# A cross-attention loop on one core: VectorE makes the low parts of the queries and the fourth maximum ahead of the transposition of probabilities

## The chip, the core and the metric

The kernel runs on one core of a Trainium2 chip. The metric is the device time of one execution in microseconds. Five engines work from queues of their own, each in the order in which the program gives it instructions: TensorE (PE; its weight loads are shown as PEld), VectorE (DVE), ScalarE (ACT), GpSimd (POOL), and SyncE (SP), which here only issues DMAs. An engine stops at an instruction whose inputs, or whose output buffer, are not ready, and everything behind it in its queue stops too.

## The reference

The input `x` is 32 batches of 512 queries with 640 channels; the context is 32 batches of 77 keys with 1024 channels. There are 20 heads of 32 channels. Only the text part of the context exists (77 keys), so the other three attentions of the source have no keys. Cut to what is computed:

```python
q = x @ to_q_w                                   # 32 x 512 x 640, 20 heads of 32
k, v = ctx @ to_k_w, ctx @ to_v_w                # 32 x 77 x 640
s = einsum('bhqd,bhkd->bhqk', q, k) / sqrt(32)
out = merge(softmax(s) @ v) @ to_out_w + to_out_b + x
```

All is float32. The kernel keeps float32 precision on PE by splitting operands into a high part (rounded to the PE's reduced format) and a low part (the remainder): three products instead of one.

## The kernel before

A first stage (some 280 us of the span) projects keys and values of all batches and stores them, split, in DRAM. Then comes the main loop of 160 *slots*: slot n works on batch b = n div 5 and on chunk j = n mod 5, that is on four heads (128 channels) and all 512 queries. The slots are pipelined by hand; the order of instructions in the code is the order in each engine's queue. `slot(n)` issues work for several chunks at once:

- **Queries of the next chunk.** `queries(n+1)` is 15 matmuls (L442) into the one PSUM bank `pq`, six between the first and second scores, nine between the second and third. `split_q(n+1)` makes the high part with ScalarE (L453), copies it to the other half of the partitions with POOL (two of L457), and makes two low parts with VectorE (two of L459). All three kinds are needed by the first scores of slot n+1.
- **Scores and exponentials of this chunk.** `scores(n, t)` for the four query tiles t = 0 to 3: three matmuls each (L477, one against `kb`, two against `kc`), and a VectorE reduction for the negated maxima (L485, "nm"). There are three score banks. `exps(n, t)`: four exponentials of ScalarE (L495), one a head, with their sums; they write the probabilities `pn` (two buffers).
- **Normalization and transposition of the chunk before.** `sums(n-1)` is a reciprocal on VectorE (L505). `normalize(n-1)` is one POOL product over all probabilities (L510). `transpose_p(n-1)` is one VectorE transposition in 32 x 32 blocks into the single buffer `z` (L517), and four SP DMAs of `z` to the scratch tensor `pd` (L524).
- **Values two slots on.** `load_p` brings `pd` back as `raw`, in another layout, with two SP DMAs (L533, L534): that of slot m + 2 brings the chunk m. In slot m + 3 `cast_p`, `rest_p` and `last_p` split it: ScalarE casts (L541, L547), a VectorE difference (L548), a POOL difference (L555). `values` is six matmuls (L569) into `pa`. `sum_a` adds the halves: a ScalarE copy (L580) and two VectorE sums (L582). In the slot after, `high_a` (ScalarE, L589) and `low_a` (VectorE, L594) split the result.
- **Output projection.** `piece` issues 24 matmuls a slot (L612) for a batch behind, in two groups, into two banks `po`. `finish` adds a closed bank to the residual with bias `xr` (VectorE, L641) and stores it (SP). The residual is loaded by SP (`load_residual`, L601, in j = 1 to 4) and gets its bias from POOL (`add_bias`, L605), in j = 2 and 3 ahead of L555, else behind the query copies.
- **Input of the next batch.** SP loads `xs` (L253, in slots j = 4), VectorE transposes it (L257, one in j = 0, two in j = 1, one in j = 2), ScalarE and POOL split it (L264, L265, two chunks in j = 2, three in j = 3).

So on VectorE a slot of the steady loop reads, before the change: maximum 0, L548, reciprocal, L594, maximum 1, xr sums, maximum 2, **transposition (L517), two low parts (L459), maximum 3**, xr sums, sums of the values (L582); with the transpositions of x where they belong. On PE: scores 0, six query matmuls, scores 1, nine query matmuls, scores 2, output projection, values, scores 3, output projection. On ScalarE: L541, L589, L547, exponentials 0 and 1, query copy (L453), exponentials 2, copies of x, L580, exponentials 3. On POOL: bias, L555, normalization, query copies, low parts of x, bias.

The flag `has_out` is true where an output projection of an earlier batch belongs to the slot (n = 7 and up); `ahead` is false only in the last slot.

Of the kernel before, what the change touches and what calls it, by code (L numbers as in the profile page):

```python
# [51 lines left out]
def kernel(  # L52
# [410 lines left out]
    def scores(n, t):  # L463
        b, j = divmod(n, NC_)
        g = GROUP_OF[j]
        qt, (kb, kc) = qts[n % 2], kbs[g]
        jg = j - GROUPS[g][0]
        sc = ps.tile([P, S], F32, tag="sc", name="sc", bufs=3)
        half = KCOLS // 2
        for m, (cols, keys_) in enumerate(  # L470
            (
                (slice(0, KCOLS), kb[:, jg]),
                (slice(0, half), kc[:, jg, 0]),
                (slice(half, KCOLS), kc[:, jg, 1]),
            )
        ):
            nc.tensor.matmul(  # L477
                sc[:, cols],
                qt[:, m, t * P : (t + 1) * P],
                keys_,  # L480
                start=(m == 0),
                stop=(m == 2),
            )
        nm = main.tile([P, HPC], F32, tag="nm", name="nm", bufs=3)
        nc.vector.tensor_reduce(  # L485
            nm, sc[:, :KCOLS].rearrange("p (h k) -> p h k", k=NKEY), AX.X, ALU.max, negate=True
        )
        return sc, nm
# [14 lines left out]
    def sums(n):  # L503
        rs = main.tile([P, NQ * HPC], F32, tag="rs", name="rs", bufs=2)
        nc.vector.reciprocal(rs, sms.pop(n))  # L505
        return rs
# [7 lines left out]
    def transpose_p(n):  # L514

        pn = pnb[n % 2]
        nc.vector.transpose(  # L517
            z.rearrange("p b t j -> p t b j"),
            pn.rearrange("p (t h) k -> p t (h k)", t=NQ).rearrange("p t (b i) -> p t b i", i=Q),
        )  # L520
        pd = dram.tile([(NBLK + 2) * Q, S], F32, tag="pd", name="pd", bufs=6)
        rows = pd[: NBLK * Q].rearrange("(b i) q -> i b q", i=Q)
        for a in range(4):
            nc.sync.dma_start(  # L524
                rows[:, :, a * P : (a + 1) * P],
                z[a * Q : (a + 1) * Q].rearrange("p b t j -> p b (t j)"),
            )
        pds[n] = pd
# [8 lines left out]
    def cast_p(n):  # L537

        raw = raws[n]
        pp = late[0].tile([P, 5, S], FPR, tag="pp", name="pp", bufs=1)  # L540
        nc.scalar.copy(pp[:, 0:2, :], raw[:, 0:2, :])  # L541
        pps[n] = pp

    def rest_p(n):

        raw, pp = raws[n], pps[n]
        nc.scalar.copy(pp[:64, 4, :], raw[:64, 2, :])  # L547
        nc.vector.tensor_tensor(  # L548
            pp[:, 2:4, :], raw[:, 0:2, :], pp[:, 0:2, :].bitcast(F32), ALU.subtract
        )  # L550

    def last_p(n):

        raw, pp = raws.pop(n), pps[n]
        nc.gpsimd.tensor_tensor(  # L555
            pp[64:, 4, :], raw[:64, 2, :], pp[:64, 4, :].bitcast(F32), ALU.subtract
        )
# [26 lines left out]
    def high_a(n):  # L584
        if n >= N - NC_ + 1:
            at = xpool[0].tile([P, 2, S], FPR, tag="xt", name="at", bufs=7)
        else:
            at = late[0].tile([P, 2, S], FPR, tag="at", name="at", bufs=8)
        nc.scalar.copy(at[:, 0, :], pas[n][:, 0])  # L589
        ats[n] = at  # L590
# [13 lines left out]
    def add_bias(b, t):  # L604
        nc.gpsimd.tensor_tensor(xrs[b, t], xrs[b, t], bias, ALU.add)  # L605
# [29 lines left out]
    def finish():  # L635

        while closed:
            b, t, h = closed.pop(0)
            xr = xrs[b, t]
            cols = slice(h * HALF, (h + 1) * HALF)  # L640
            nc.vector.tensor_tensor(  # L641
                xr[:, cols], pos.pop((b, t, h))[:, :HALF], xr[:, cols], ALU.add
            )
            if (b, t) == (B - 1, NQ - 1):
                nc.sync.dma_start(out[b, t * P : (t + 1) * P, cols], xr[:, cols])
            elif h == 1:
                nc.sync.dma_start(out[b, t * P : (t + 1) * P, :], xr)
# [23 lines left out]
    def refill(b, j, part):  # L671

        heads = range(2 * part, 2 * part + 2)
        segments = SEGMENTS[4 * part : 4 * part + 4]
        if j == 0:
            load_keys(b, 1, heads)
        elif j == 1:
            load_values(b, 0, segments)
        elif j == 2 and b + 1 < B:
            load_keys(b + 1, 0, heads)  # L680
        elif j == 3:
            load_values(b, 1, segments)

    def slot(n, beside=()):
        b, j = divmod(n, NC_)
        ahead, more = n + 1 < N, b + 1 < B
        back, first = PIECES[j]
        bo_, has_out = b - back, b >= back
        xsplits = SPLIT_X.get(j, ((), ())) if more and n > LATE else ((), ())
        turns = TRANSPOSE_X.get(j, ((), (), ())) if more and b else ((), (), ())  # L690
        if b == 1 and j < 2:
            turns = (((), (), ()), ((0, 1), (2,), ()))[j]
        taken = takes.get(n)

        filling = taken is not None and not has_out
        if not filling:
            refill(b, j, 0)
        if taken is not None:
            cast_p(taken)
        if n - 1 in takes:  # L700
            high_a(takes[n - 1])
        bias_now = j in BIAS and b >= BIAS[j][0]
        if bias_now and (j in (2, 3) or not ahead):
            add_bias(b - BIAS[j][0], BIAS[j][1])
        s = scores(n, 0)
        if taken is not None:
            rest_p(taken)
        rs = sums(n - 1) if n else None
        if taken is not None:
            last_p(taken)  # L710
        if n:
            normalize(n - 1, rs)
        if n - 1 in takes:
            low_a(takes[n - 1])
        exps(n, 0, *s)
        if ahead:
            queries(n + 1, 0, 2)
        s = scores(n, 1)
        if n - LAG + 1 in pds and n > LATE:
            load_p(n - LAG + 1)  # L720
        if filling:
            refill(b, j, 0)
        if n == NC_:
            load_x(b + 1, (2, 3))
        for k in WO.get(n, ()):
            nc.sync.dma_start(wos[0][:, k].bitcast(F32), wo_dram[:, k].bitcast(F32))
        refill(b, j, 1)
        finish()
        if j == 4 and b and b + 2 < B:
            load_x(b + 2, (0, 1))  # L730
        if j in RESIDUAL and b >= RESIDUAL[j][0]:
            load_residual(b - RESIDUAL[j][0], RESIDUAL[j][1])
        exps(n, 1, *s)
        for i in turns[0]:
            transpose_x(b + 1, i)
        if ahead:
            queries(n + 1, 2, NC_)
        s = scores(n, 2)
        if not ahead:
            exps(n, 2, *s)  # L740
            piece(bo_, first)
            s = scores(n, 3)
        early = ahead and has_out and j in (0, 3)
        if early:
            piece(bo_, first)
            finish()
        if n and has_out:
            transpose_p(n - 1)
        if ahead:
            split_q(n + 1)  # L750
            if bias_now and j not in (2, 3):
                add_bias(b - BIAS[j][0], BIAS[j][1])
            exps(n, 2, *s)
        if n and not has_out:
            transpose_p(n - 1)
        if j == 4 and b + 2 < B:
            load_x(b + 2, (0, 1) if not b else (2, 3))
        for c in xsplits[0]:
            split_x(b + 1, c)
        if not ahead:  # L760
            exps(n, 3, *s)
            normalize(n, sums(n))
            finish()
            piece(bo_, first + 1)
            values(taken)
            sum_a(taken)
            return
        if has_out:
            if not early:
                piece(bo_, first)  # L770
        else:
            s = scores(n, 3)
        if taken is not None:
            values(taken)
        if len(beside) > 0:
            context_values(LAST, beside[0], psv)
        if has_out:
            s = scores(n, 3)
        finish()
        for i in turns[1]:  # L780
            transpose_x(b + 1, i)
        if taken is not None:
            sum_a(taken)
        for c in xsplits[1]:
            split_x(b + 1, c)
        exps(n, 3, *s)
        if len(beside) > 1:
            context_values(LAST, beside[1], psv)
        if has_out:
            piece(bo_, first + 1)  # L790
        for i in turns[2]:
            transpose_x(b + 1, i)
# [141 lines left out]
```

## Time and profile before

| | |
|---|---|
| median of the runs | 2037.02 us (3 runs, 2031.57 to 2038.48) |
| profiled execution | 2031.54 us |
| its span, first to last instruction | 2029.8 us |
| granted PE clock, mean | 0.992 |
| PE busy | 1913.5 us (94%) |
| PE weight loads busy | 1677.6 us (83%) |
| VectorE busy | 1559.7 us (77%) |
| ScalarE busy | 1533.9 us (76%) |
| POOL busy | 1237.7 us (61%) |
| DMA moved | 437.69 MB, 216 GB/s in the mean |

The lines of a profile name the line of the kernel, the engine, the operation and its tiles. A group's line gives the number of instructions, their busy time, the mean time of one, and the idle time of the engine in front of them with what ended it. A line of the waits gives who waited for whom: total us, number of waits, the longest. A line of the timeline gives the start in us from the span's beginning, the duration, the engine, the line, the operation with its tiles, how many instructions are merged, and in brackets the idle time before with its releaser. "issue" stands where the profile shows no releaser. Matmuls overlap in their pipelines, so two starts say more than one duration.

### The profile page before, as it was taken

The numbers are of one execution on the slowest core, as the hardware profiler recorded it, in microseconds if no ns is written. First come the engines' busy times: TensorE is split into PE (matmuls) and PEld (weight loads), VectorE is DVE, ScalarE is ACT, GpSimd is POOL, SyncE is SP. The second block draws the span as 40 slices with busy tenths as digits, with TensorE's granted clock in tenths as the row PEclk, the third lists the DMA queues.
The fourth block names the chain that finished last, engine by engine and source line by source line (L and its number), as shares of the span: only waits on it lengthen the run. The fifth ranks groups of instructions, "written<-read, shape, count | busy, mean of one in ns | idle before, by whom it ended". The sixth has DMA issues, their size and how long they took to land.

```text
span 2029.8 us, 37658 instructions
## 1 busy us (share of the span) xinstructions
PE 1913.5 (94%) x10332; PEld 1677.6 (83%) x10332; DVE 1559.7 (77%) x2494; ACT 1533.9 (76%) x6210; POOL 1237.7 (61%) x1030
## 2 busy tenths in 40 slices
PE   9999997999999999999999999999999999999998
PEld 7787886788888888888888888888888888888887
DVE  4444346788888888888888888888888888888885
ACT  3232237888888888888888888888888888888883
POOL 1201156676667766766666667766776667666663
PEclk9999999999999999999999999999999999999999
DMA  9878878888888888889888888888888888889875
GB/s 187 183 178 228 192 185 209 217 225 223 218 226 220 219 225 225 229 216 230 219 219 225 215 230 226 217 226 224 226 225 223 217 226 217 223 218 233 225 195 161
DMA packets 586305, 437.69 MB, mean 216 GB/s; under 512 B 212400, under 2 KB 494448, under 8 KB 586096
## 3 DMA queue, kind: packets, MB, share of 16 engines
q1 hardware_dynamic: 580944, 420.78, 82.7%
q0 software_dynamic: 5056, 14.34, 2.6%
q8 instruction: 85, 1.39, 0.3%
q14 instruction: 124, 1.02, 0.2%
q10 hardware_dynamic: 96, 0.16, 0.0%
HBM read 253.48 MB, written 181.64 MB: 214 GB/s over the span
## 4 chain that ended last, share of the span: by engine, by line
POOL 24%; DVE 19%; DMA 18%; issue 13%; ACT 12%; PE 11%; SPq 3%; DVEq 0%; POOLq 0%; ACTq 0%
POOL pn L510 14%; POOL pp L555 9%; PE pk L191 6%; DVE qt L459 6%; DMA raw<-pd 5%; DMA pd<-z 5%; ACT pn L495 4%; DVE z L517 4%; DMA xs<-in_x_dram 3%; DVE pa L582 3%; ACT pp L541 3%; PE pv L191 3%; DVE nm L485 2%; ACT at L589 2%; DMA out_dram<-xr 2%
## 5 line engine op out<-in xcount | busy, mean ns | idle before, releaser
L495 ACT ACTIVATE pn<-sc,nm 128x77 f32<-128x77 f32 x2560 | 802.8, 335 | 227.5 <-DVE nm L485 221.3
L612 PE MATMUL po<-wo_s,at 128*128 128x320 f32 x3840 | 641.6, 315 | 5.9 <-DVE xr L641 3.1
L442 PE MATMUL pq<-xt,wq_s 128*128 128x512 f32 x2400 | 620.3, 399 | 0.0
L612 PEld LDWEIGHTS po<-wo_s,at 128*128 128x128 f32 x3840 | 569.8, 190 | 17.8 <-DVE xr L641 6.8
L495 ACT ACTIVATION_READ_ACCUMULATOR pn<-sc,nm 128x1 f32 x2560 | 546.0, 213 | 0.0
L442 PEld LDWEIGHTS pq<-xt,wq_s 128*128 128x128 f32 x2400 | 429.7, 190 | 76.1
L555 POOL TENSOR_TENSOR pp<-raw,pp 64x512 fp32r<-64x512 f32 x160 | 216.2, 1352 | 387.6 <-ACT pp L547 279.3
L517 DVE STREAM_TRANSPOSE z<-pn 128x1280 f32<-128x1280 f32 x160 | 241.9, 1512 | 205.2 <-POOL pn L510 205.1
L510 POOL TENSOR_TENSOR pn<-pn,rs 128x1232 f32<-128x1232 f32 x160 | 364.4, 2277 | 14.2 <-DVE rs L505 1.8
L477 PE MATMUL sc<-kc,qt 128*128 128x154 f32 x1280 | 257.8, 263 | 79.8 <-DVE qt L459 50.4
L477 PEld LDWEIGHTS sc<-kc,qt 128*128 128x128 f32 x1280 | 218.4, 188 | 131.6 <-issue 69.3
L485 DVE TENSOR_REDUCE nm<-sc 128x4 f32<-128x308 f32 x640 | 291.5, 464 | 14.1 <-PE sc L477 8.8
L605 POOL TENSOR_TENSOR xr<-xr,bias 128x640 f32<-128x640 f32 x128 | 200.5, 1568 | 112.6 <-DMA xr<-in_x_dram 86.1
L569 PE MATMUL pa<-pp,vb 128*128 128x512 f32 x960 | 252.0, 397 | 4.4 <-POOL pp L555 3.0
L582 DVE TENSOR_TENSOR pa<-pa,aw 64x512 f32<-64x512 f32 x320 | 222.5, 695 | 21.6 <-ACT aw L580 11.2
L548 DVE TENSOR_TENSOR pp<-raw,pp 128x1024 fp32r<-128x1024 f32 x160 | 198.1, 1238 | 40.8 <-ACT pp L541 40.7
L265 POOL TENSOR_TENSOR xt<-xs,xt 128x512 fp32r<-128x512 f32 x160 | 202.6, 1285 | 36.7 <-ACT xt L264 28.8
L459 DVE TENSOR_TENSOR qt<-pq,qt 64x512 fp32r<-64x512 f32 x320 | 214.5, 670 | 9.5 <-ACT qt L453 4.6
L457 POOL CAST qt<-qt 64x512 fp32r<-64x512 f32 x320 | 195.4, 611 | 19.7
L477 PE MATMUL sc<-kb,qt 128*128 128x308 f32 x640 | 195.9, 306 | 9.0 <-ACT pn L495 4.3
L569 PEld LDWEIGHTS pa<-pp,vb 128*128 128x128 f32 x960 | 173.7, 188 | 35.1 <-POOL pp L555 3.9
L580 ACT COPY aw<-pa 64x1024 f32<-64x1024 f32 x160 | 161.9, 1012 | 17.4 <-PE pa L569 13.6
(48 smaller groups left out, 1820.7 us busy)
## 6 DMA issues: line engine op xcount, KB each, us to landing
pd<-z SPq DMA_DIRECT2D x640, 160.0 KB, 3.3
raw<-pd SPq DMA_DIRECT2D x160, 512.0 KB, 4.1
xs<-in_x_dram SPq DMA_DIRECT2D x128, 320.0 KB, 5.9
xr<-in_x_dram SPq DMA_DIRECT2D x128, 320.0 KB, 3.8
out_dram<-xr SPq DMA_DIRECT2D x127, 320.0 KB, 3.7
raw<-pd SPq DMA_DIRECT2D x160, 128.0 KB, 4.3
v_dram<-vs SPq DMA_DIRECT2D x80, 192.0 KB, 4.1
kc<-k_dram SPq DMA_DIRECT2D x128, 57.8 KB, 4.2
```

The costliest lines, as they stand in the source:

```text
L265: low.tensor_tensor(parts[1], src, parts[0].bitcast(F32), ALU.subtract)
L442: nc.tensor.matmul(pqs[n], wq_s[:, k, a, j * P : (j + 1) * P], xts[b, k][:, c, :], start=(k == 0 and m == 0), stop=(k == NC_ - 1 and m == 2),)
L459: nc.vector.tensor_tensor(qt[r, 1 + w, :], pq[r], qt[r, 0, :].bitcast(F32), ALU.subtract)
L477: nc.tensor.matmul(sc[:, cols], qt[:, m, t * P : (t + 1) * P], keys_, start=(m == 0), stop=(m == 2),)
L485: nc.vector.tensor_reduce(nm, sc[:, :KCOLS].rearrange("p (h k) -> p h k", k=NKEY), AX.X, ALU.max, negate=True)
L495: nc.scalar.activation(pnb[n % 2][:, at, :NKEY], sc[:, i * NKEY : (i + 1) * NKEY], AF.Exp, bias=nm[:, i : i + 1], accum_out=sms[n][:, at : ...
L510: nc.gpsimd.tensor_tensor(pf, pf, rs.unsqueeze(2).to_broadcast([P, NQ * HPC, NKEY]), ALU.mult)
L517: nc.vector.transpose(z.rearrange("p b t j -> p t b j"), pn.rearrange("p (t h) k -> p t (h k)", t=NQ).rearrange("p t (b i) -> p t b i", i=Q),)
L555: nc.gpsimd.tensor_tensor(pp[64:, 4, :], raw[:64, 2, :], pp[:64, 4, :].bitcast(F32), ALU.subtract)
L569: nc.tensor.matmul(pas[n][:, p, :], vb[:, p, t, :], pp[:, c, :], start=(c == p), stop=(t == 1),)
L582: nc.vector.tensor_tensor(pa[64 * p : 64 * p + 64, 0], pa[:64, p], aw[:, p], ALU.add)
L612: nc.tensor.matmul(pos[b, t, h][:, :HALF], ats[b * NC_ + j][:, a, t * P : (t + 1) * P], wos[0][:, j, c, h * HALF : (h + 1) * HALF], start= ...
```

## The change

In the slots where `has_out` holds, `transpose_p(n-1)` moves from in front of `split_q(n+1)` to behind `scores(n, 3)`. VectorE's order there becomes: maximum 2, two low parts, maximum 3, transposition, xr sums, x transposition, sums of the values. The four stores of `z` move with it in SP's queue: in slots j = 4 they pass two loads of `xs`; elsewhere they keep their place among SP's issues. The last slot keeps its order, and so do the slots without an output projection (n below 7). The other engines' queues are unchanged.

```diff
         if early:
             piece(bo_, first)
             finish()
-        if n and has_out:
+        if not ahead:
             transpose_p(n - 1)
         if ahead:
             split_q(n + 1)
...
         if has_out:
             s = scores(n, 3)
+            transpose_p(n - 1)
         finish()
         for i in turns[1]:
             transpose_x(b + 1, i)
```

## The prediction

> **What bounds the kernel now.** I read the page first: PE is called busy for 94% of the span, VectorE (DVE) 77%, ScalarE (ACT) 76%, GpSimd (POOL) 61%. Its chain of waits nevertheless gives PE 11% and POOL 24%, so something else times the loop. The list of waits, second, says who holds whom:
>
> ```profile
> DVE z L517 <- POOL pn L510: 205.1, 155, 5.1
> ACT pn L495 <- DVE nm L485: 221.3, 287, 3.3
> PE sc L477 <- DVE qt L459: 50.4, 126, 0.9
> ```
>
> VectorE waits 1.3 us in each slot for the normalization before its transposition; what is queued behind (low parts of the queries, fourth maximum) is what PE and ScalarE wait for. Third, the timeline of one slot with j = 4, engine by engine (start, duration, engine, line; in brackets the idle time before it and its releaser):
>
> ```profile
> 1024.15 1.28 POOL L555 TENSOR_TENSOR pp<-raw,pp 64x512 fp32r<-64x512 f32 x1 [1.56 <-issue]
> 1025.51 2.28 POOL L510 TENSOR_TENSOR pn<-pn,rs 128x1232 f32<-128x1232 f32 x1
> 1034.57 1.29 POOL L555 TENSOR_TENSOR pp<-raw,pp 64x512 fp32r<-64x512 f32 x1 [3.78 <-ACT pp L547]
> ...
> 1027.82 1.51 DVE L517 STREAM_TRANSPOSE z<-pn 128x1280 f32<-128x1280 f32 x1 [1.66 <-POOL pn L510]
> 1029.26 1.37 DVE L459 TENSOR_TENSOR qt<-pq,qt 64x512 fp32r<-64x512 f32 x2
> 1030.66 0.48 DVE L485 TENSOR_REDUCE nm<-sc 128x4 f32<-128x308 f32 x1
> 1031.69 1.42 DVE L582 TENSOR_TENSOR pa<-pa,aw 64x512 f32<-64x512 f32 x2
> ...
> 1031.17 0.33 ACT L495 ACTIVATE pn<-sc,nm 128x77 f32<-128x77 f32 x1 [1.68 <-DVE nm L485]
> 1032.39 1.06 ACT L541 CAST pp<-raw 128x1024 fp32r<-128x1024 f32 x1
> 1033.33 0.61 ACT L589 CAST at<-pa 128x512 fp32r<-128x512 f32 x1
> 1033.80 0.63 ACT L547 CAST pp<-raw 64x512 fp32r<-64x512 f32 x1
> ...
> 1030.02 0.30 PE L477 MATMUL sc<-kb,qt 128*128 128x308 f32 x1
> 1030.77 0.31 PE L477 MATMUL sc<-kc,qt 128*128 128x154 f32 x1 [0.37 <-DVE qt L459]
> 1030.92 1.59 PE L442 MATMUL pq<-xt,wq_s 128*128 128x512 f32 x6
> ```
>
> Start to start these rows close a ring: L555 1.36, normalization 2.31, transposition 1.44, two low parts 1.40, fourth maximum 0.51, four exponentials 1.22, L541 0.94, L589 0.47, L547 0.77, and L555 again: 10.42 us. The slots measured from first score matmul to first score matmul last 10.41, 10.59, 10.53, 11.25 and 10.30 us for j = 0 to 4 (medians), 53.31 us a batch in the mean. So the ring is the clock, and PE has slack: without its two stops at the scores of the next chunk the PE row takes 1.43 + 0.32 + 2.12 + 0.32 + 1.80 + 1.41 + 0.33 + 1.79 for the pieces from 1020.50 to 1030.02, and 0.33 for the scores: 9.85 us.
>
> **The change, part by part.** No instruction is added or dropped. The order of PE, ACT and POOL stays; VectorE's and SyncE's (SP's) changes in the 152 slots n = 7 to 158.
>
> *Low parts and fourth maximum earlier.* They leave the ring: 1.40 + 0.51 = 1.91 us. What is left through POOL (L555, normalization, transposition, sums L582, L589, L547) is 1.36 + 2.31 + 1.44 + 1.34 + 0.47 + 0.77 = 7.7 us, plus 0.5 for an xr sum and 0.85 for an x transposition where they stand between: at most 9.1, no bound any more. Four candidates are next, per slot:
> - PE: 9.85, 49.25 a batch.
> - A VectorE-ScalarE ring: sums 1.34, maximum 0.45, L548 1.14, reciprocal 0.16, L594 0.55, maximum to exponentials 0.50, four exponentials 1.22, query copy 0.62, low parts 1.40, maximum 0.51, transposition 1.44: 9.33. Behind the transposition j = 1 and 4 have an xr sum (0.5), j = 0 and 1 an x transposition (0.85): 10.2, 10.7, 9.3, 9.3, 9.8, or 49.3 a batch. PE tolerates lag here: with 9.85 us slots L555 would end some 4.7 us after a slot's first score matmul, and the values that need it start at 6.3 (1026.49 - 1019.72, less the stop of 0.45). Those 1.6 us let long and short slots even out.
> - The residual. In j = 1 its load (L601) is issued behind two sets of values, these behind raw, this behind the pd of slot j = 0. From the end of that transposition to the bias sum (L605) of j = 2 it is 13.85 us in the median (12.75 to 15.13). L605 stands ahead of L555 and the normalization: 13.85 + 1.57 + 1.36 + 2.31 + 1.51 = 20.6 us for two slots, 0.9 over PE's 19.7.
> - The trip of the probabilities. z ends, four pd issues, landing, raw issue (5.2 to 7.0 us after z's end), 4.2 us landing: 9.4 to 11.5. Then 1.06 (L541) + 1.14 + 0.16 + 0.55 + 0.50 + 1.22 + 0.62 + 1.40 + 0.51 + 1.51 = 8.67 to the end of the transposition two slots on: 18.1 to 20.2 per two slots, under 2 x 9.85 but for j = 4.
>
> *Transposition later.* It no longer finds the normalization late (it follows the fourth maximum, which waits for PE's fourth scores). Behind it on VectorE stand the xr sums, x transpositions and the two sums; relative to the slot they move little, as lows and maximum were ahead of them before too, and the 1.3 us of idle time goes. Its four pd issues move with it on SP. In j = 4 they are moved past two xs loads (0.85 us each to issue), which now go out first; behind pd wait output stores, keys or values, and raw. Today L541 starts 13.5 to 14.2 us after z ends; in a 9.85 us slot I estimate 9.6 to 10.8: the transposition ends 10.1 us into its slot (fourth scores at 8.05, maximum, transposition), and L541 can follow at 19.7, or at 20.9 without delaying L589, which waits for the sums. So the cover is used up in j = 4 (trip 11.5) and nearly in j = 0, at nothing to 0.9 us a batch.
>
> *A collision.* Where L548 (two SBUF inputs) meets a bias sum on POOL, one waits for the other:
>
> ```profile
> 1066.28 1.57 POOL L605 TENSOR_TENSOR xr<-xr,bias 128x640 f32<-128x640 f32 x1 [1.08 <-DMA xr<-in_x_dram]
> 1066.95 1.98 DVE L548 TENSOR_TENSOR pp<-raw,pp 128x1024 fp32r<-128x1024 f32 x1 [0.52 <-ACT pp L541]
> 1068.04 2.02 POOL L555 TENSOR_TENSOR pp<-raw,pp 64x512 fp32r<-64x512 f32 x1 [0.20 <-ACT pp L547]
> ```
>
> L548 is 1.98 instead of 1.23: it got through 1.08 us after L605's end at 1067.85. In the tighter slots j = 2 and 3 the two come nearer to each other; the price lies between nothing and 1.57 us in each, 0 to 3.1 a batch. I take 0.6 for both together, near the low end: eight of the 160 L548 rows are over 1.3 us today, and the 1.6 us of tolerance absorb the first part.
>
> [...] Taken at a full bias sum in both slots it would make the batch 53.4 us, and the change worth nothing.
>
> The sum: 49.4 (PE and the second ring, nearly equal) + 0.9 (residual) + 0.6 (collisions) = 50.9 a batch; the trip's 0 to 0.9 is left to the range, since it lies in other slots beside the same tolerance. Against 53.31: 2.4 x 152/5 = 73 us. From the profiled execution's 2031.54 us that gives 1958.5; the runs' median lies 5.5 above that execution (2037.02), so 1964.
>
> [...]
>
> **The rivals.**
> 1. *PE alone bounds it.* No residual, no collision: 53.31 - 49.25 = 4.06 x 30.4 = 123, 1914. For it: PE's pieces stand end to end today. Against it: POOL waits 86.1 us for the residual in 29 slots already.
> 2. *The trip is the ring.* DMA engines are 0.88 busy in the mean and 1.06 to 1.13 in slots j = 0; the same bytes in a shorter slot land later. With 12 us everywhere: (12 + 8.67)/2 = 10.33, a gain of (10.66 - 10.33) x 152 = 50 us: 1987. For it: j = 4 shows 11.5 already. Against it: j = 2 and 3 show 9.4.
> 3. *Slower: the trip, past its point.* The transposition behind the fourth maximum starts the pd writes later; from a trip of 2 x 10.66 - 8.67 = 12.65 us on, ScalarE waits for raw longer than before, and all behind L541 with it. At 14 us (the gap that j = 1 has today) a slot takes 11.33: 102 us more, 2139. Against it: raw is late 6 times today, 4.0 us in all.
> 4. *It does nothing.* The fourth maximum now waits for PE's fourth scores ahead of the transposition; should that wait take up all of the 1.3 us, the slot stays at 10.66. Against it: PE has those scores 2.4 us before the maximum reads them (1028.2 and 1030.66).
>
> **How the numbers follow.** Forecast (1930 to 1980) 0.58; rival 1 0.10; rival 2 (1980 to 2025) 0.14; no change 0.04; rival 3 0.14. Less than 0.3% (6 us) can't be told from no change here. Faster 0.82, same 0.04, slower 0.14. The range reaches from rival 1's side (1918) into rival 2 (2012), and leaves out the no-change and slower cases and a little at either end.
>
> **What would show it.** Right: VectorE's wait for pn at L517 falls from 205 us to under 60; PE's waits for qt at L459 go; the second-order waits are L605 for its load and L541 for raw; slots j = 0, 3, 4 take 9.8 to 10.2 us, the pair j = 1, 2 at least 20.6; PE busy nears 97%. Wrong: L541 waiting for raw in most slots (rivals 2 and 3), or PE's waits for qt as before.

## The result, and the profile after

The changed kernel takes 2067.03 us in the median of four runs (2062.03 to 2067.76); the kernel before, on the same chip, 2035.92 (2031.57 to 2038.48). The ratio is 1.015, with a 95% interval of 1.0125 to 1.0174: 31 us slower, where 73 us faster were forecast. The profiled execution of the changed kernel took 2062.03 us, its span 2060.2, its mean granted PE clock was 0.976 (0.992 before). The page's first part:

```profile
PE 1924.0 (93%) x10332; PEld 1686.9 (82%) x10332; DVE 1601.8 (78%) x2494; ACT 1538.7 (75%) x6210; POOL 1289.8 (63%) x1030
```

The list of waits answers to the one of before (engine and line that waits, for whom, total us, times, longest):

```profile
POOL xr L605 <- DMA xr<-in_x_dram: 109.4, 36, 8.5
ACT pp L541 <- DMA raw<-pd: 93.6, 33, 5.4
ACT pn L495 <- DVE nm L485: 80.3, 164, 2.6
PE po L612 <- DVE xr L641: 65.7, 30, 4.4
DVE pp L548 <- ACT pp L541: 65.5, 81, 3.8
DVE z L517 <- POOL pn L510: 15.4, 40, 2.9
```

The ring of before is open: L517 waits 15.4 us for the normalization instead of 205.1, ScalarE 80.3 us for maxima instead of 221.3, and PE's score matmuls wait 1.7 us behind L459 instead of 50.4. In its place stands ScalarE's wait for `raw` at L541: 93.6 us, where the trace of before has 4.0. It comes 33 times, about once a batch, and PE's stop for the bank that L641 has to empty (65.7 us, before 3.1) comes 30 times.

The slots, from first score matmul to first score matmul (means in us over the batches b = 4 to 30, counted from 0), say where:

| | j = 0 | j = 1 | j = 2 | j = 3 | j = 4 | batch |
|---|---|---|---|---|---|---|
| before | 10.41 | 10.70 | 10.54 | 11.34 | 10.31 | 53.31 |
| after | 9.83 | 13.24 | 10.10 | 11.12 | 10.16 | 54.46 |

Four slots give 1.39 us a batch, as the opened ring should; j = 1 takes 2.54. The net 1.15 over 30.4 batches is 35 us, near the measured 31. In j = 1 ScalarE's wait for `raw` is 3.05 us a batch.

The timeline of one such place follows; slot j = 4 begins at 1576.26, j = 0 at 1586.48, j = 1 at 1596.32, j = 2 at 1612.01 (start, duration, engine, line; in brackets the idle time before it with its releaser):

```profile
1586.21 1.51 DVE L517 STREAM_TRANSPOSE z<-pn 128x1280 f32<-128x1280 f32 x1
1603.81 1.23 DVE L548 TENSOR_TENSOR pp<-raw,pp 128x1024 fp32r<-128x1024 f32 x1 [3.76 <-ACT pp L541]
1606.04 0.48 DVE L641 TENSOR_TENSOR xr<-po,xr 128x320 f32<-128x320 f32 x1
...
1585.15 0.95 SPq L253 DMA_DIRECT2D xs<-in_x_dram  x2
1587.75 3.11 SPq L524 DMA_DIRECT2D pd<-z  x4
1595.86 0.38 SPq L533 DMA_DIRECT2D raw<-pd  x1
...
1602.73 1.04 ACT L541 CAST pp<-raw 128x1024 fp32r<-128x1024 f32 x1 [5.10 <-DMA raw<-pd]
...
1582.94 1.57 PE L569 MATMUL pa<-pp,vb 128*128 128x512 f32 x6
1600.83 1.52 PE L612 MATMUL po<-wo_s,at 128*128 128x320 f32 x9
1606.57 1.17 PE L612 MATMUL po<-wo_s,at 128*128 128x320 f32 x3 [4.22 <-DVE xr L641]
1607.54 2.50 PE L569 MATMUL pa<-pp,vb 128*128 128x512 f32 x6
```

The transposition of slot j = 4 ends at 1587.72. The `xs` loads have been issued by then, the `pd` writes go out at once, but the first load of `raw` can be issued only 8.14 us later, and L541 starts 15.01 us after the transposition's end. ScalarE was free 5.10 us before that. Behind L541 stand L548 on VectorE, behind L548 the residual sum L641, behind L641 the PE bank of L612: PE stops for 4.22 us, and six value matmuls after it take 2.50 us where the same six took 1.57 in the slot j = 4.

The DMA view of 1584 to 1596 (tile, issuing queue, number, KB each, median us from issue to landing) gives the length of the trip:

```profile
xs<-in_x_dram SPq DMA_DIRECT2D x3, 320.0 KB, 7.6
pd<-z SPq DMA_DIRECT2D x4, 160.0 KB, 6.7
raw<-pd SPq DMA_DIRECT2D x1, 512.0 KB, 6.8
```

Over the whole loop `pd` lands in 3.5 us and `raw` in 4.1. This place is one of the longest; in the mean over the batches (b = 5 to 30, here and below) the first `raw` of slot j = 4 goes out 8.59 us after the transposition's end (7.02 before the change), and L541 begins 4.37 us later, 12.96 in all.

The kernel before has the same long trip, and there hardly a wait shows it. One such place, with the DMA view of its `raw` in the third row:

```profile
602.13 1.51 DVE L517 STREAM_TRANSPOSE z<-pn 128x1280 f32<-128x1280 f32 x1 [1.66 <-POOL pn L510]
610.38 0.39 SPq L533 DMA_DIRECT2D raw<-pd  x1
raw<-pd SPq DMA_DIRECT2D x1, 512.0 KB, 6.2
617.12 1.06 ACT L541 CAST pp<-raw 128x1024 fp32r<-128x1024 f32 x1
```

The transposition ends at 603.64 and `raw` lands 12.9 us later, but ScalarE is busy until L541 starts, 13.5 us after that end, so no wait stands in brackets. The means, in us from the transposition's end in slot j = 4:

| | `raw` issued | `raw` landed | ScalarE free for L541 | its wait for `raw` |
|---|---|---|---|---|
| before | 7.02 | 13.25 | 13.52 | 0.16 |
| after | 8.59 | 12.87 | 9.90 | 3.05 |

The change has not lengthened this trip. It has taken away 3.6 us of the cover, the time in which ScalarE is still at other work while the trip runs. In the other four slots of the kernel before, `raw` has landed after 9.3 to 10.7 us, 3.1 to 4.4 us before ScalarE is free.

The view by windows of the same stretch of the changed kernel, and of the stop and what follows it, has busy time of each engine, then the granted PE clock, the DMA engines' share and GB/s:

```profile
1584.00:1594.00 10.00, 10.00 (x60) 9.04 (x59) 8.52 (x14) 8.89 (x39) 6.70 (x6) 1.00 1.13 256
1600.00:1606.50 6.50, 2.35 (x15) 1.97 (x14) 2.74 (x7) 3.61 (x14) 1.51 (x2) 0.98 0.75 150
1606.50:1612.00 5.50, 5.43 (x24) 4.92 (x25) 4.08 (x7) 4.55 (x23) 3.24 (x3) 0.72 0.94 262
```

PE is busy throughout the first window and the DMA share is 1.13 (above 1, so the times of its packets overlap): the place in the batch where the DMA engines have most to do. The mean share is 1.13 in the slots j = 0 and 0.75 to 0.87 in the others; before the change it was 1.09 and 0.80 to 0.84. In the second PE works 2.35 of 6.50 us; in the third its clock is 0.72.

### The profile page after: what moved, and what is told of

Its sections match the earlier page's. It is cut to its first block, busy times and chain, and to the rows that moved or that the text cites. A ratio compares the mean times of both kernels' runs of the same rounds, so it can differ in the third digit from the quotient of the medians.

```text
span 2060.2 us, 37687 instructions
## 1 busy us (share of the span) xinstructions
PE 1924.0 (93%) x10332; PEld 1686.9 (82%) x10332; DVE 1601.8 (78%) x2494; ACT 1538.7 (75%) x6210; POOL 1289.8 (63%) x1030
## 3 DMA queue, kind: packets, MB, share of 16 engines
q8 instruction: 85, 1.39, 0.3%
## 4 chain that ended last, share of the span: by engine, by line
ACT 25%; DVE 24%; DMA 17%; PE 8%; issue 4%; SPq 4%; POOL 3%; DVEq 0%; POOLq 0%; ACTq 0%
ACT pn L495 12%; DMA pd<-z 8%; DVE pp L548 7%; DMA raw<-pd 6%; DVE z L517 4%; ACT pp L541 4%; DVE nm L485 4%; ACT xt L264 3%; PE po L612 3%; ACT aw L580 3%; DVE at L594 3%; DVE qt L459 3%; SPq L524 2%; PE pq L442 2%; ACT qt L453 2%
## 5 line engine op out<-in xcount | busy, mean ns | idle before, releaser
L495 ACT ACTIVATE pn<-sc,nm 128x77 f32<-128x77 f32 x2560 | 802.2, 334 | 87.1 <-DVE nm L485 80.3
L612 PE MATMUL po<-wo_s,at 128*128 128x320 f32 x3840 | 648.7, 317 | 79.0 <-DVE xr L641 65.7
L612 PEld LDWEIGHTS po<-wo_s,at 128*128 128x128 f32 x3840 | 575.1, 191 | 92.5 <-DVE xr L641 74.0
L442 PE MATMUL pq<-xt,wq_s 128*128 128x512 f32 x2400 | 627.8, 401 | 4.3 <-POOL xt L265 2.2
L555 POOL TENSOR_TENSOR pp<-raw,pp 64x512 fp32r<-64x512 f32 x160 | 236.5, 1478 | 318.2 <-ACT pp L547 296.4
L605 POOL TENSOR_TENSOR xr<-xr,bias 128x640 f32<-128x640 f32 x128 | 229.0, 1790 | 159.8 <-DMA xr<-in_x_dram 109.4
L459 DVE TENSOR_TENSOR qt<-pq,qt 64x512 fp32r<-64x512 f32 x320 | 220.4, 689 | 117.7 <-ACT qt L453 112.6
L569 PE MATMUL pa<-pp,vb 128*128 128x512 f32 x960 | 275.9, 419 | 12.6 <-POOL pp L555 9.4
L548 DVE TENSOR_TENSOR pp<-raw,pp 128x1024 fp32r<-128x1024 f32 x160 | 232.7, 1454 | 66.0 <-ACT pp L541 65.5
L517 DVE STREAM_TRANSPOSE z<-pn 128x1280 f32<-128x1280 f32 x160 | 241.9, 1512 | 37.5 <-DMA pd<-z 17.0
L477 PE MATMUL sc<-kc,qt 128*128 128x154 f32 x1280 | 231.3, 260 | 13.1 <-POOL qt L457 11.0
L541 ACT CAST pp<-raw 128x1024 fp32r<-128x1024 f32 x160 | 168.7, 1055 | 95.0 <-DMA raw<-pd 93.6
L569 PEld LDWEIGHTS pa<-pp,vb 128*128 128x128 f32 x960 | 181.0, 198 | 57.1 <-POOL pp L555 26.4
L265 POOL TENSOR_TENSOR xt<-xs,xt 128x512 fp32r<-128x512 f32 x160 | 205.3, 1304 | 34.8 <-ACT xt L264 28.5
```

The lines of the kernel that those rows point to most:

```text
L442: nc.tensor.matmul(pqs[n], wq_s[:, k, a, j * P : (j + 1) * P], xts[b, k][:, c, :], start=(k == 0 and m == 0), stop=(k == NC_ - 1 and m == 2),)
L459: nc.vector.tensor_tensor(qt[r, 1 + w, :], pq[r], qt[r, 0, :].bitcast(F32), ALU.subtract)
L477: nc.tensor.matmul(sc[:, cols], qt[:, m, t * P : (t + 1) * P], keys_, start=(m == 0), stop=(m == 2),)
L495: nc.scalar.activation(pnb[n % 2][:, at, :NKEY], sc[:, i * NKEY : (i + 1) * NKEY], AF.Exp, bias=nm[:, i : i + 1], accum_out=sms[n][:, at : ...
L517: nc.vector.transpose(z.rearrange("p b t j -> p t b j"), pn.rearrange("p (t h) k -> p t (h k)", t=NQ).rearrange("p t (b i) -> p t b i", i=Q),)
L548: nc.vector.tensor_tensor(pp[:, 2:4, :], raw[:, 0:2, :], pp[:, 0:2, :].bitcast(F32), ALU.subtract)
```

## Experiments

Times are medians of a run's group; each ratio is against the kernel before on the same chip, with its 95% interval. "After" and "before" name the kernel that an edit starts from.

**The order on SyncE, or the trip itself.** The first theory was the order of the issues: with the change two `xs` loads go out ahead of the `pd` writes in j = 4. The second was the length of the trip through DMA engines with a share of 1.13 in j = 0. e1 gives the changed kernel the old order, e2 gives the kernel before the new one and nothing else; in e3 only the low parts go ahead of the transposition, and the fourth maximum stays behind it.

```diff
# e1, from after
-        if j == 4 and b + 2 < B:
+        if j == 4 and b + 2 < B and not has_out:
             load_x(b + 2, (0, 1) if not b else (2, 3))
...
             transpose_p(n - 1)
+            if j == 4 and b + 2 < B:
+                load_x(b + 2, (2, 3))
# e2, from before
+        if j == 4 and b + 2 < B and has_out:
+            load_x(b + 2, (2, 3))
         if n and has_out:
             transpose_p(n - 1)
...
-        if j == 4 and b + 2 < B:
+        if j == 4 and b + 2 < B and not has_out:
# e3, from before
-        if n and has_out:
+        if not ahead:
             transpose_p(n - 1)
         if ahead:
             split_q(n + 1)
+            if has_out:
+                transpose_p(n - 1)
```

> The changed kernel, with the two xs loads of slots j = 4 put back behind the four pd stores in SP's queue. Theory 1 (SP's order: the xs loads that got ahead of pd lengthen the trip of the probabilities of slot j = 4, which ScalarE then awaits in j = 1): L541's wait for raw falls from 93.6 us to under 30, raw is issued about 7 us after z's end in j = 4 (8.5 now), slot j = 1 falls from 13.2 us to under 11, and the time is 1960 to 1990. Rival (the transposition simply comes too late, whatever SP's order): raw is still awaited for over 60 us, slot j = 1 stays over 12.3, 2035 to 2065.

> The kernel before, with VectorE's order as it was, and only SP's order of the change: in slots j = 4 the two xs loads go out ahead of the pd stores. Theory 1: the trip of j = 4 grows from some 11.5 us to 13.5 to 15.4 while L541 comes 13.5 us after z's end, so j = 1 loses 0 to 2 us a batch and the time rises to 2050 to 2095. Rival (the transposition's lateness alone): within 10 us of before, since z is as early as it was.

> The kernel before, with only the two low parts of the queries ahead of the transposition; the fourth maximum stays behind it, and SP's order is that of before. Theory 1: the ring is shorter by 1.40 us and the trip keeps its SP order, so nearly all of the gain comes: 1955 to 1985. Rival: the transposition is still later than before, raw is awaited over 60 us, 2030 to 2060. If the fourth maximum is what must come first, the time lies between, about 2010.

| run | us | ratio | j = 0 to 4 | batch |
|---|---|---|---|---|
| e1 | 2057.19 | 1.0129 (1.011 to 1.0147) | 9.84 13.27 9.93 11.14 10.05 | 54.23 |
| e2 | 2053.62 | 1.0109 (1.0087 to 1.0132) | 10.39 11.42 10.53 11.44 10.29 | 54.07 |
| e3 | 2034.74 | 1.0017 (1.0003 to 1.0031) | 9.84 12.38 10.01 11.29 9.87 | 53.39 |

e1 leaves j = 1 at 13.27 and the wait for `raw` at 95.3 us: in the changed kernel the order of the issues is not the cause, and the first theory falls. `raw` is indeed issued earlier there (7.03 us after the transposition's end of j = 4 in the mean, instead of 8.59), but L541 then begins 6.06 us later instead of 4.37: the sum is 13.09 where it was 12.96. Yet the order is not free: by itself, in e2, it costs 1.1%. That is inside the range that the first theory gave for e2, but by luck, for the way is another: ScalarE waits 1.5 us in all for `raw` there, while the transposition of slot j = 0 waits for the `pd` writes of j = 4, which still read the single buffer `z`:

```profile
DVE z L517 <- DMA pd<-z: 44.2, 17, 3.8
```

The kernel before has no such wait, the changed kernel 17.0 us. e3 gains as much in four slots as the whole change (1.59 us a batch) and loses 1.68 in j = 1, where `raw` lands after 13.07 us and ScalarE is free after 11.87: the two cancel. Its time lies in the range of its rival, though `raw` is awaited for 39.8 us and not for over 60.

**Which transposition pays.** In e11 the changed order holds only in slots j = 1, 2, 3, in e12 only in j = 4.

```diff
# e11 with (1, 2, 3), e12 with (4,), from after
-        if not ahead:
+        if not ahead or (has_out and j not in (4,)):
             transpose_p(n - 1)
...
             s = scores(n, 3)
-            transpose_p(n - 1)
+            if j in (4,):
+                transpose_p(n - 1)
```

> The change in slots j = 1, 2 and 3 alone; in j = 4 and 0 the transposition stays ahead of the low parts. Theory 2: the trip of j = 4 starts as early as before (9.6 us into its slot), so raw is in time in j = 1; j = 4 and 0 stay at 10.3 and 10.4, j = 1 to 3 get 10.5, 10.0, 11.1: 52.3 a batch, 2000 to 2012, faster than before. Rival (every slot's order matters alike): about 2050.

> The change in slots j = 4 alone. Theory 2: the one late transposition whose probabilities are awaited in j = 1, so most of the loss with none of the gain: slot j = 1 12 to 13 us, time 2060 to 2090. Rival: one slot in five, a fifth of the loss: 2037 to 2045.

e11 takes 2038.45 us (1.0027, 1.001 to 1.0043; 10.73 11.16 10.00 11.61 10.01, batch 53.50), e12 2047.33 (1.0071, 1.0052 to 1.009; 9.84 12.14 10.43 11.29 10.30, batch 53.99). e12 has half of the loss with one slot in five, but not through `raw`, for which ScalarE waits 0.3 us in all: as in e2, the transposition of j = 0 waits for `z`, 50.3 us. e11 shows no gain: against the kernel before its j = 2 and 4 win 0.84 us, and j = 0, 1 and 3 lose 1.05; ScalarE waits 18.2 us for `raw`. Both times lie outside their ranges, and the two runs don't show what each slot's order is worth by itself.

**Fewer bytes in the full stretch.** e9 leaves out the second pair of `xs` loads from the third batch on (0.66 MB a batch), e10 does the same to the kernel before; e6 is e1 without the eight key loads of slot j = 0. In these kernels those batches compute with old input or keys.

```diff
# e9 from after, e10 from before
-        if j == 4 and b + 2 < B:
+        if j == 4 and b + 2 < B and b < 2:
...
-            xss[b] = xpool[0].tile([P, S // Q, C // 4], F32, tag="xs", name="xs")
+            xss[b] = xss[b - 1] if b > 3 else xpool[0].tile([P, S // Q, C // 4], F32, tag="xs", name="xs")
# e6, from e1
-        if j == 0:
+        if j == 0 and b < 2:
             load_keys(b, 1, heads)
```

> The changed kernel without the second pair of xs loads in slots j = 4 from the third batch on (half of the channels keep old data): 0.66 MB a batch less in the DMA engines, exactly where the trip of slot j = 4 starts. Theory 2 (the trip is too long because raw lands behind those bytes, whatever the order): raw lands some 11 us after z's end, slot j = 1 falls from 13.2 to 10.5 us, time 1975 to 1990, well below before. Rival (it is not the trip but PE's and VectorE's new order): 2040 or more.

> The kernel before without the same loads, as a control. Its ring does not hold the trip, so theory 2 expects only the rare waits for raw to go: 2018 to 2032. If the bytes themselves bound both kernels, it falls as much as the changed one.

> As the first experiment, and the eight key loads of slots j = 0 are left out from the third batch on (the keys of chunks 2 to 4 stay those of an earlier batch). SP has 4 us less to issue and the DMA engines 0.35 MB less. Theory 2: raw goes out 5.2 us after z's end and lands sooner too, so slot j = 1 falls by 2 us or more, time 1985 to 2010. Rival (full DMA engines): the time falls by the bytes alone, 3% of a batch's 11.84 MB, under 15 us: 2040 to 2057.

| us | with the loads | without them |
|---|---|---|
| order of before | 2035.92 | 2024.55 (e10: 0.9962, 0.9946 to 0.9978) |
| order of after | 2067.03 | 1990.97 (e9: 0.9791, 0.9765 to 0.9816) |

The table is the test of the second theory. With the loads the new order costs 31 us, without them it brings 34; by the ratios, which compare runs on one chip, the loads themselves cost the old order 8 us and the new one 73. Without them `raw` lands 10.36 us after the transposition's end in e9 and 10.63 in e10, so they lengthen the trip by some 2.6 us in either order. In e10 ScalarE is free only after 13.48 us, in e9 after 9.88. In e9 the slots are 9.84 10.38 10.10 11.66 9.96 (51.93), L541 follows the transposition of j = 4 after 10.45 us (mean), and ScalarE's wait is

```profile
ACT pp L541 <- DMA raw<-pd: 20.9, 23, 2.9
```

e6 says the same of the keys: 2000.06 us (0.9839, 0.9822 to 0.9856), j = 1 at 10.91, L541 11.68 us after the transposition of j = 4. It has no run of the old order beside it.

**Reordering the issues inside the stretch.** e5 is e1 with the four key loads that stood ahead of `raw` put behind it; e8 does that to e3.

```diff
# e5 from e1, e8 from e3
-        if not filling:
+        if not filling and j:
             refill(b, j, 0)
...
-        if filling:
+        if filling or j == 0:
             refill(b, j, 0)
```

> The changed kernel with the xs loads behind the pd stores (as the first experiment), and in slots j = 0 the four key loads that stood ahead of raw in SP's queue behind it. Theory 2 (the trip of the probabilities from the transposition of slot j = 4 to L541 of slot j = 1, 13.1 us in the first experiment, is what PE waits for in j = 1): raw goes out 5.2 us after z's end instead of 7.0, the wait for raw falls from 3.3 to about 1.5 us a batch, slot j = 1 from 13.3 to about 11.5, and the time from 2057 to 2000 to 2015. Rival (DMA engines full: the landing grows by what the issue gains): slot j = 1 over 12.8, 2045 to 2060.

> Only the low parts ahead of the transposition (the maximum behind it), and the four key loads of j = 0 behind raw. Theory 2: slot j = 1 falls from 12.4 to about 10.8, time from 2035 to 1980 to 1995, faster than before. Rival (full DMA engines): 2025 to 2037.

e5: 2056.26 us (1.0115, 1.008 to 1.0149), 9.83 12.46 10.83 10.99 10.33, batch 54.44. `raw` goes out 5.66 us after the transposition instead of 7.03 (means), and L541 begins 6.84 instead of 6.06 us later: more than half of what the issue gained the landing lost, and 0.8 us went from j = 1 into j = 2, where POOL now waits 4.69 us for the residual. e8: 2061.54 (1.0135, 1.0107 to 1.0164), 9.84 11.20 11.66 11.69 9.96, batch 54.35: j = 1 better, j = 2 worse, the same residual wait (4.65), and slower than e3. Neither gains, and e8 is slower than both of its ranges; the loads have to leave the stretch, not only change their place in it.

**What follows the late `raw`.** e7 is e1 with `finish()`, the residual sum that frees the PE bank, ahead of the slot's first scores, so that it is not queued behind L548. e4 is e1 with the bias sums of j = 2 and 3 moved behind the query copies, which should remove the collision of L605 and L548.

```diff
# e7, from e1
+        finish()
         s = scores(n, 0)
# e4, from e1
-        if bias_now and (j in (2, 3) or not ahead):
+        if bias_now and not ahead:
             add_bias(b - BIAS[j][0], BIAS[j][1])
...
             split_q(n + 1)
-            if bias_now and j not in (2, 3):
+            if bias_now:
                 add_bias(b - BIAS[j][0], BIAS[j][1])
```

> As the first experiment, and VectorE makes the xr sum that frees PE's output bank ahead of the first maximum of a slot instead of behind L548, the reciprocal, L594 and the second maximum. In j = 1 PE then no longer waits for raw through L548 and the xr sum, but first at the values matmuls, through L555. Theory 2 with the stop of PE as its price: PE's wait at L612 in j = 1 (2.2 us a batch) turns into a wait of about 1 us at L569, a gain of 0.5 to 1.5 us a batch: 2012 to 2042. If the bank is no part of it: 2050 to 2062.

> As the first kernel, and the bias sums of slots j = 2 and 3 behind the query copies on POOL, as in j = 0 and 4. If the residual's load and the collisions of L605 with L548 still cost time in j = 2 and 3: L548's mean falls from 1.45 us to 1.25, slot j = 3 from 11.1 to 10.3 us and the time lies 15 to 40 us below the first kernel's. If they are hidden: within 8 us of it.

e7: 2045.38 us (1.0062, 1.0041 to 1.0083), 9.84 11.43 11.13 11.71 9.89, batch 54.0. The wait for `raw` stays; PE's long stop goes:

```profile
ACT pp L541 <- DMA raw<-pd: 105.0, 36, 4.6
PE po L612 <- DVE at L594: 52.8, 55, 2.1
```

In j = 1 L612 no longer waits for L641 (2.17 us a batch in e1); a shorter wait of the value matmuls L569 for L594 (1.22) stands in its place. Against e1 that is some 12 us (14 by the ratios), and the stretches of half PE clock fall from 20 to 4 (mean granted clock of the profiled executions 0.976 in e1, 0.988 in e7); how much of the gain is the clock and how much the stop itself, this run does not separate. e4 missed: 2055.62 (1.0116, 1.0098 to 1.0135), 9.84 13.59 9.82 10.57 10.64, batch 54.45. The mean of L548 does not fall (1460 ns; 1407 in e1), and what j = 3 gains j = 1 and 4 lose.

**The same bytes at another time.** e13 leaves nothing out: the second pair of `xs` is loaded in j = 0 behind `raw` instead of in j = 4, and x's transpositions stand one place later. e14 does it to the kernel before, e15 to e3.

```diff
# e13 from after, e14 from before, e15 from e3
-        if b == 1 and j < 2:
+        if b and more and j < 2:
             turns = (((), (), ()), ((0, 1), (2,), ()))[j]
...
-        if n == NC_:
+        if j == 0 and b and b + 1 < B:
             load_x(b + 1, (2, 3))
...
-        if j == 4 and b + 2 < B:
-            load_x(b + 2, (0, 1) if not b else (2, 3))
+        if n == 4:
+            load_x(b + 2, (0, 1))
```

> The changed kernel with the second pair of xs loads of every batch issued in the next slot, j = 0, behind raw (all is loaded), and the x transpositions one place later (two in the middle of j = 1, one at the end of it or in j = 2). If the bytes cost only where the trip of j = 4 runs: the wait for raw in j = 1 falls under 1.5 us a batch, slot j = 1 to 10.5 to 11.5, time 1985 to 2015, faster than before. If they cost wherever they are moved, because the DMA engines as a whole set the pace: 2040 to 2065.

> Control: the kernel before with the same move of the xs loads. Its ring of 10.4 us a slot stays, so 2022 to 2040 by either theory; more only if the later x transpositions lengthen the ring in j = 1 (0.85 us a batch, up to 2055).

> Only the low parts ahead of the transposition, and the xs loads moved as in the first run. The transposition is earlier by the wait for PE's fourth scores, so more room for the trip: 1980 to 2010, no slower than the first run. If it is slower by over 10 us, the maximum has to come early as well.

| run | us | ratio | j = 0 to 4 | batch |
|---|---|---|---|---|
| e13 | 2020.0 | 0.9939 (0.9919 to 0.9959) | 9.83 9.97 11.84 10.93 10.30 | 52.87 |
| e14 | 2030.04 | 0.9994 (0.9981 to 1.0006) | | 53.24 |
| e15 | 2023.13 | 0.996 (0.9947 to 0.9972) | 9.84 10.48 10.85 11.87 10.0 | 53.04 |

The move by itself is worth nothing (e14); with it the new order is 10 us faster than the old instead of 31 slower. j = 1 falls from 13.24 to 9.97, its wait for `raw` from 3.05 us to 0.5, for `raw` now lands 10.37 us after the transposition's end. In e14 it lands after 10.58, and ScalarE is free after 13.48. e13 and e15 are still slower than expected, by 5 and 13 us at least. j = 2 is now the late one: POOL waits for the residual, as the prediction's second-order term said.

**All three moves.** e16 is e13 with `finish()` first, e17 is e16 with the bias sums behind the query copies, e18 is e17's three moves with VectorE's old order.

> As the first run, with the xr sum that frees PE's bank ahead of the first maximum. If PE's stop at the bank is still a cost: 8 to 20 us below the first run. If raw is in time, the bank is free in time too: within 6 us of it.

> As the run before with moved xs loads and early xr sum, and the bias sums of j = 2 and 3 behind the query copies on POOL, so that the residual's load no longer stands ahead of L555 and the normalization. If the residual is what is left: slot j = 2 falls from 11.9 to 10.2 to 10.8 us, 1955 to 1985. If raw's own lateness in j = 2 (1.6 us a batch) holds it: 2000 to 2015.

> Control: the same three moves with VectorE's order of before (transposition ahead of the low parts). Its ring of 10.4 us a slot remains: 2015 to 2040.

| run | us | ratio | batch |
|---|---|---|---|
| e16 | 2013.77 | 0.9916 (0.9901 to 0.9931) | 52.69 |
| e17 | 1996.51 | 0.9838 (0.9818 to 0.9858) | 52.2 |
| e18 | 2051.31 | 1.0112 (1.0087 to 1.0137) | 54.09 |

e17 beats both kernels, the one before by 31 us; it lies between its two ranges. Its slots are 9.83 9.84 10.51 11.39 10.63. The lists of waits of e17, then of e18:

```profile
ACT pp L541 <- DMA raw<-pd: 65.3, 53, 3.2
PE po L612 <- DVE at L594: 42.7, 50, 1.1
DVE z L517 <- POOL pn L510: 3.9, 3, 3.4
```

```profile
ACT pn L495 <- DVE nm L485: 250.5, 287, 2.6
DVE z L517 <- POOL pn L510: 214.6, 154, 2.1
```

e18 has the ring of before again, 214.6 us at L517. With the same three moves on both sides the two orders are 55 us apart. But not all of that is gain: e18 is 24 us slower than the kernel before on the same chip, and above its range. In the old order the moves cost time (slot j = 0 takes 10.98 us instead of 10.41), though the move of the loads alone did not (e14); which of the other two does it was not separated. Against the kernel before, the order with its moves is worth 31 us.

## Why the prediction was wrong

- **The ring: right.** 205.1 us at L517 became 15.4 (under 60 was forecast), PE's waits for the low parts went, and where nothing else is late a slot takes PE's pieces: j = 0 measured 9.83, forecast 9.85. e9 against e10 (34 us) and e17 against the kernel before (31 us) show what is left of the 73 us once the trip is covered.
- **The trip of the probabilities: the step that failed.** The prediction gave it 9.4 to 11.5 us, let L541 follow 9.6 to 10.8 after the transposition, and priced the rest at "nothing to 0.9 us a batch". The cover was right, with some luck: ScalarE is free after 9.90 us, though the transposition ends 11.28 us into its slot and not 10.1. The trip was mis-sized. To the issue of `raw`, read slot by slot (up to 7.0 us, in j = 4), the prediction added one landing for all slots, 4.2 us, near the loop's median of 4.1. In its own trace the `raw` of j = 4 lands 6.23 us after its issue in the mean, 13.25 us after the transposition. Set against a cover of 9.9 that would have said a wait of 3.4 us a batch; 3.05 was measured. What hid it was the short list of waits: `raw` was late only 6 times because the old ring kept ScalarE from L541 for 13.5 us. The prediction itself quoted a DMA share of up to 1.13 in j = 0, the slot that this trip passes through, under rival 2, and did not let it lengthen the term. That the trip is long because of the bytes in that stretch is shown by taking them away (e9, e6) and by moving them (e13), with the old order beside it for the `xs` loads (e10, e14).
- **The tolerance: wrong with it.** The prediction left the trip out of the sum "since it lies in other slots beside the same tolerance", 1.6 us that let long and short slots even out. A wait of 3.05 us is more than that, and it reached PE: through L548, queued ahead of L641, to the bank (65.7 us at L612). With PE at the 9.85 us of its pieces in j = 0 (9.83 measured) and near them in j = 2 and 4 (10.10, 10.16), little is left to win the time back. e7, which lets L641 pass, regained some 12 to 14 us.
- **Rivals 2 and 3.** Rival 2 let the same bytes land later in a shorter slot; on the trip from j = 4 they did not (12.87 us after, 13.25 before). Rival 3 had the right mechanism at the wrong place: it had ScalarE wait for `raw` in every slot from a trip of 12.65 us on, at 2139 us, and held against it that `raw` was late only 6 times, which measured the old cover and not the trip. It needed only one slot in five: j = 1 holds all of the loss in the table of slots. It had a chance of 0.14, and should have been priced by itself for the slot with a DMA share of up to 1.13.
- **SyncE's order: not the cause in the changed kernel.** The prediction named the two `xs` issues that go out ahead of `pd`, 0.85 us each. They do not hold `pd` back on the queue: in the place shown they are over at 1586.10, ahead of the transposition's end. The writes land later, though: the slowest of the four takes 7.19 us in the mean, 4.68 before, so `raw` goes out later (8.59 us after the transposition's end, 7.02 before), and then lands sooner (4.28 us after its issue, 6.23 before). By itself the new order costs 1.1% in the kernel before (e2), through `z`; taking it back in the changed one leaves j = 1 where it was (e1).
- **The residual: right, but hidden.** POOL waits 109.4 us for `xr` (86.1 before). Its 0.9 us a batch became a bound only where the trip was covered: j = 2 takes 11.84 in e13, and 10.51 in e17, where the bias sum no longer stands ahead of L555.
- **The collision: a larger term than taken.** The mean of L548 rose from 1238 to 1454 ns, and 46 of its 160 rows are over 1.3 us (8 before): 0.216 x 160 = 34.6 us, or 1.1 a batch against 0.6. Each of the 46 met a POOL operation and ended 1.08 us after that one's end (1.075 to 1.086): 34 times a low part of x (L265), 12 times a bias sum (L605), as all eight of before (1.079 to 1.086). Since e4 neither shortened L548 nor the loop, how much of it is on the path stays open.
- **Slot j = 3** was forecast at 9.8 to 10.2 and measured 11.12. It is over 10.5 in every run whose slots are given above, also in e17, where PE stops 1.09 us a batch there for L594. The prediction's four candidates leave out that ScalarE is busy for 10.44 us of this slot in the trace of before, and POOL for 9.78 (10.39 and 10.16 after the change); three of the five input splits stand in it. Whether that sets the slot, no run isolates. It matters for the number: in e9, with the trip nearly covered, a batch takes 51.93 us against the forecast's 50.9, and the run 1991 us, still above the range.
- **PE near 97%** did not come about: 93%.

A second buffer for `xs`, which would let its loads go out in any slot, was not tried; nor was the clock by itself.

## What to carry to other kernels

Before a step moves later on one engine, measure the DMA round trip that it starts in each slot by itself, from the step's end to the landing, and compare it with the cover that the new order leaves in that slot. A median over the loop hides the one slot that matters: `raw` lands in 4.1 us in the median, and in 6.2 us in the mean of slot j = 4. A short list of waits is no proof of a short trip either: here 4.0 us of waits stood over a trip of 13.25 us with 0.3 us to spare. Where the opened ring brings the main engine near the sum of its own pieces, as here (9.83 us measured in j = 0, 9.85 the sum), one late arrival in a batch is hardly made up: j = 1 lost 2.54 us a batch, and the other four slots won back 1.39. And a change that loses can still be the right one: with the loads moved out of the stretch and two smaller moves, the same order gained 31 us on the kernel before.

## What the runs showed of the hardware

**The PE clock after a stop.** Between 360 and 1980 us of the span the clock record of before has one stretch at half clock, of 3.4 us; the changed kernel has 17, each of 3.4 or 6.8 us, 64.8 us together. 15 of the 17 begin within 1.6 us of the end of a stop of PE at L612, of 1.86 to 4.39 us; three stops of that length (2.38, 2.56 and 3.06 us) have none near their end. After the stop of 4.22 us shown above three L612 took 1.17 us, where three took 0.70 after the stop of 3.06 us, and six L569 2.50 instead of 1.57: 1.4 us on top of the stop in these rows alone. If PE had been the bound in all of the 64.8 us they would have cost 32, an upper end. By that estimate half clock alone can explain at most 32 of 2062 us here, 1.6%, and the measured share is unknown.

**Landing took what issue gained.** The trip from j = 4, which runs through the slot with a mean DMA share of 1.13 in the changed kernel, hardly depended on the order of its issues: 8.59 + 4.37 = 12.96 us in the changed kernel, 7.03 + 6.06 = 13.09 in e1, 5.66 + 6.84 = 12.50 in e5 (issue of `raw` after the transposition, and from there to L541; means). To the landing alone the kernel before has 7.02 + 6.23 = 13.25. Without the second pair of `xs` it is 6.13 + 4.32 = 10.45 to L541 (e9).
